# Making the rotary tables on GpSimd, and copying the first sequence's turned tokens on ScalarE, in a macaron block

## The chip, the cores and the metric

The kernel runs on one core of a Trainium2 chip. A core has five engines that run side by side, each through its own list of instructions in a fixed order: TensorE (PE: matrix products and transposes, with its weight loads shown apart as PEld), VectorE (DVE), ScalarE (ACT), GpSimd (POOL) and SyncE (SP), which here only issues DMAs. An engine waits for another by semaphores. Products land in PSUM, eight banks of 128 x 512 float32; everything else stands in SBUF, whose 128 partitions are the rows of every tile.

The metric is the device time of one execution in microseconds (us). Before the change it is 1862.89, the median of three runs (1862.62 to 1865.09).

## The reference

Eight sequences of 512 tokens with 128 channels pass through a macaron block: half an FFN block, an attention with latent keys, and the same FFN block by half again.

```python
x = x + 0.5 * ffn(layernorm(x))
x = x + latent_attention(layernorm(x))       # 16 heads of 8
x = x + 0.5 * ffn(layernorm(x))

def layer(x, ...):                           # ffn runs two of these
    h = shift_token(x)                       # second half of the channels from one token before
    q, k, v = split(h @ wqkv)                # 8 heads of 64
    q = l2norm(q) * qs;  k = l2norm(k) * ksc
    q, k = rotary_xpos(q, k)                 # q*cos*scale + rotate_half(q)*sin*scale; k by 1/scale
    x = x + local_attention(q, k, v) @ wo    # windows of 64, each sees itself and the one before
    h = layernorm(shift_token(x)) * lg + lb
    a, g = split(h @ w1 + b1)
    return x + (a * gelu(g)) @ w2 + b2
```

All of it is float32.

## The kernel before

The kernel has three parts: `ffn("f0")`, the first FFN half with two layers; `latent_attention()`; and `ffn("f1")`, the second FFN half. In an FFN half each of the 16 pairs of a layer `l` and a sequence `b` goes through `shift` (the tokens are normalized in layer 0, transposed, and copied with the channels' second half one token later), then for each of its four blocks `i` of 128 tokens through `begin`, `turn`, `scores`, `turn_probabilities`, `values` and `residual`, and at the end through `feed_forward`.

**Order by a planner.** Nothing of an FFN half is issued where it is written. Each piece of work is a step with a kind, an engine, a cost in microseconds, a rank, and what it reads, writes and holds. `Plan.run` (L159) then simulates the five engines: it looks at the 110 steps of the main row with the lowest ranks (and 40 of each side row), works out when each could start by the costs, takes the engine that can start first, and gives it, among its steps that can start by then, the one with the lowest rank. The order in which steps are picked is the order in each engine's list. The rank of a step is 100 times its place in the sequence of blocks (block `i` of the sequence numbered `s` has place 4s + i) plus an offset by kind from `PLACE` (L23). A step that needs a result of another engine starts 0.2 us later than it, with 0.1 more behind a PSUM access. The plan doesn't know the time of the first load, 5.4 us on the chip.

**The first steps.** The planner's steps that the prediction speaks of are these, with offset and planned cost:

- `ist`, `inr`, `inn`, `ina`: statistics on DVE (L488 to L490), an inverse root on ACT (L471, L472), a correction of it on POOL (L475 to L478) and the four normalizing products on DVE (L496), which write Y.
- `sh` (-500): four transposes of Y into one PSUM bank on PE (L508).
- `sd` (-790, DVE, 0.62): the bank's first 64 rows into the tile hT (L524). `sp`: a column of zeros on POOL. `sa` (-690, ACT, 0.5): the other 64 rows, one column later (L532).
- `qk0`, `qk1`, `v` (-320, -240, -19, PE): the projections of hT (L546), each into a bank of its own. There are four such banks.
- `sq0`, `sq1` (-480, -390, ACT): squares of a projection (L572), for the norm.
- `cs0`, `cs1` (-570, -360, DVE, 1.25): the two rotary products, with the cosine table (L556) and with halves exchanged by the sine table (L559). They read the bank and the table `("tab", l, s)`.
- `ad0`, `ad1` (-190, -430, POOL, 1.28): their sum (L580).
- `tb` (-450, DVE, 1.2): a rotary table. There are four, by layer `l` and by `t` for queries and keys; each multiplies the constant rotary factors, 128 x 256, by the heads' scale (L350), and the sine factors in two halves of 128 x 128 (L354). Their place is 2l, so the ranks are -450 for layer 0 and -250 for layer 1. All four read the tile `tables_u`, into which SP loads the scales and the rotary factors (L985, L990; 512 KB for the latter).
- `ld` at place 4 and `lw` (rank 100): once `tables_u` is free, its room, the only buffer of the ring `r_u`, takes seven small weights of the latent stage (L1027). Six products on PE (L1041) and their copies on DVE (L1047) make three matrices of them.

At the end of the first half, the first steps of the latent stage (`latent_begins`) are planned into the last sequences as a side row: memsets, projections, and DMAs that spread heads over partitions (`spread`, L1275). They borrow buffers of the FFN, among them the ring `ge` of the Gelu's results.

Of the kernel before, what the change touches and what calls it, by code (L numbers as in the profile page):

```python
# [188 lines left out]
def kernel(  # L189
# [21 lines left out]
    nc = tc.nc  # L211
# [35 lines left out]
    def load_tokens(b):  # L247
        nc.sync.dma_start(out=X[:, b], in_=x[b].rearrange("(n p) c -> p n c", p=P))
# [9 lines left out]
    def load_layer(l):  # L258

        yield lambda: nc.sync.dma_start(  # L260
            out=wo_sb[l], in_=wo[l].rearrange("(n p) c -> p n c", p=P)
        )
        yield lambda: nc.sync.dma_start(out=w1_sb[l], in_=w1[l])
        for c in range(NHC):
            yield lambda c=c: nc.sync.dma_start(
                out=w2_sb[l][: hsz[c], c], in_=w2[l, c * P : c * P + hsz[c], :]
            )
        yield lambda: nc.sync.dma_start(out=b2_sb[l], in_=b2[l].partition_broadcast(P))
# [54 lines left out]
    def mask_parts():  # L323

        for name, pattern, sign, op, fill in MASKS:
            yield lambda name=name: nc.gpsimd.memset(masks[name], 0.0)
            for g in range(4):
                rows = masks[name][quadrant(g)]
                yield lambda rows=rows, pattern=pattern, sign=sign, op=op, fill=fill: (
                    nc.gpsimd.affine_select(  # L330
                        out=rows, in_=rows, pattern=pattern, compare_op=op, fill=fill, base=0,
                        channel_multiplier=sign,
                    )
                )
        for k in range(2):
            yield lambda k=k: nc.gpsimd.memset(rows_sb[:, k], float(k))
# [10 lines left out]

    def rotary_table(l, s, rot_sb, scales):
        t, g = tabs[l], scales[:, s, l]
        nc.vector.tensor_mul(  # L350
            t[:, 2 * s], rot_sb[:, 2 * s], g.unsqueeze(1).to_broadcast([P, NB, DH])
        )
        for lo, fr in ((0, HD), (HD, 0)):
            nc.vector.tensor_mul(  # L354
                t[:, 2 * s + 1, :, lo : lo + HD],
                rot_sb[:, 2 * s + 1, :, lo : lo + HD],
                g[:, fr : fr + HD].unsqueeze(1).to_broadcast([P, NB, HD]),
            )
# [46 lines left out]
    def flat(t):  # L405
        return t.rearrange("p a b -> p (a b)") if len(t.shape) == 3 else t
# [5 lines left out]
    def ffn(tagname, last):  # L412
        plan = Plan(tc, nc)

        def step(kind, engine, cost, at, *args, **kw):
            return plan.step(kind, engine, cost, 100 * at + PLACE[kind], *args, **kw)

        PE, ACT, DVE, POOL, SP = range(5)
# [63 lines left out]
        def norm(k, w, src, dst, reads, writes, slots):  # L482

            st, mv, rs, ns, nt = (Slot(r) for r in (r_st, r_mv, r_rs, r_ns, r_nt))

            def stats():
                for i in range(NB):
                    nc.vector.bn_stats(st[:, i], src()[:, i])  # L488
                    nc.vector.bn_aggr(mv[:, i], st[:, i])
                nc.vector.tensor_scalar(rs.tile, mv[:, :, 1], LN_EPS, None, ALU.add)  # L490

            first, newton = root(rs, ns, nt)

            def apply():
                for i in range(NB):
                    nc.vector.tensor_scalar(  # L496
                        dst()[:, i], src()[:, i], mv[:, i, 0:1], ns[:, i : i + 1],
                        ALU.subtract, ALU.mult,
                    )

            step(w + "st", DVE, 1.6, k, stats, reads, [rs], [st, mv, rs] + slots)
            step(w + "nr", ACT, 0.45, k, first, [rs], [ns], [rs, ns])
            step(w + "nn", POOL, 0.9, k, newton, [rs, ns], [(ns, 1)], [rs, ns, nt])
            step(w + "na", DVE, 1.15, k, apply, [(ns, 1)] + reads, writes, [mv, ns] + slots)

        def transposes(src, dst):
            for i in range(NB):
                nc.tensor.transpose(dst[:, i * P : (i + 1) * P], src(i), ident)  # L508
# [3 lines left out]
        def shift(l, b, k):  # L512

            y = [("Y", b, i) for i in range(NB)]
            if l == 0:
                norm(k, "i", lambda: X[:, b], lambda: Y[:, b], [("X", b)], y, [])
            tp, hT = Slot(mm), Slot(r_hT)
            half = C // 2
            step(
                "sh", PE, 0.5, k, lambda: transposes(lambda i: Y[:, b, i], tp),  # L520
                y + ([("W", l)] if l else []), [tp], [tp], 0.1,
            )
            step(
                "sd", DVE, 0.62, k, lambda: nc.vector.tensor_copy(hT[:half, :], tp[:half, :]),  # L524
                [tp], [(hT, 0)], [tp, hT], 0.1,
            )
            step(
                "sp", POOL, 0.1, k, lambda: nc.gpsimd.memset(hT[half:, 0:1], 0.0),
                [], [(hT, 1)], [hT],
            )  # L530
            step(
                "sa", ACT, 0.5, k, lambda: nc.scalar.copy(hT[half:, 1:T], tp[half:, 0 : T - 1]),  # L532
                [tp], [(hT, 2)], [tp, hT], 0.1,
            )
            seqs[l, b] = hT, Slot(r_kT), Slot(r_V2), Slot(r_V)
# [429 lines left out]
        def load_step(k, what, writes=(), slots=(), after=3.0):  # L965
            step("ld", SP, 0.5, k, what, [], writes, slots, after)

        def first_loads():

            tables_u = Slot(r_u)  # L970
            size = 4 * NB * DH

            def rotary():
                return flat(tables_u.tile)[:, :size].rearrange(
                    "p (f n d) -> p f n d", f=4, n=NB
                )

            def scales():
                return flat(tables_u.tile)[:, size : size + 2 * L * DH].rearrange(
                    "p (s l d) -> p s l d", s=2, l=L  # L980
                )

            for t, scale in enumerate((q_scale, k_scale)):
                load_step(
                    0, lambda t=t, scale=scale: nc.sync.dma_start(  # L985
                        out=scales()[:, t].rearrange("p l d -> p (l d)"),
                        in_=scale.rearrange("l d -> (l d)").partition_broadcast(P),
                    ), [tables_u], [tables_u],
                )
            load_step(0, lambda: nc.sync.dma_start(out=rotary(), in_=rot), [tables_u], [tables_u])  # L990
            for l in range(L):
                for t in range(2):
                    step(
                        "tb", DVE, 1.2, 2 * l,
                        lambda l=l, t=t: rotary_table(l, t, rotary(), scales()),
                        [tables_u], [("tab", l, t)], [tables_u],
                    )
            load_step(0, lambda: nc.sync.dma_start(out=cols_sb, in_=cols), [("W", 0)])
            for what in load_layer(0):
                load_step(1, what, [("W", 0)])  # L1000
            for b in range(1, B):
                load_step(NB * b, lambda b=b: load_tokens(b), [("X", b)])
            load_step(
                NB * 3, lambda: nc.sync.dma_start(out=wqkv_sb[1], in_=wqkv[1]), [("W", 1)]
            )
            for what in load_layer(1):
                load_step(NB * 4, what, [("W", 1)])
            latent_weights()
            for what in mask_parts():
                step("lb", POOL, 0.65, 5, what, [], ["masks"])  # L1010
# [224 lines left out]
        if last:  # L1235
            plan.row = 0
            latent_ends()
            plan.row = 1
        else:
            first_loads()  # L1240
        for s, (l, b) in enumerate([(l, b) for l in range(L) for b in range(B)]):
            shift(l, b, NB * s)
            for i in range(NB):
                at = (l, b, i, NB * s + i)
                begin(*at)
                turn(*at)
                scores(*at)
                turn_probabilities(*at)
                values(*at)
                residual(*at)  # L1250
            feed_forward(l, b, NB * s)
# [418 lines left out]
```

## Time and profile before

| | |
|---|---|
| median of three runs | 1862.89 us |
| the profiled execution: time, span | 1861.75, 1860.0 us |
| busy share of the span: PE, PEld, DVE, ACT, POOL | 94%, 63%, 74%, 75%, 53% |
| mean granted PE clock | 0.982 |
| PE busy in the stretches 0 to 50, 50 to 100, 100 to 150, 150 to 200 us | 28.39, 45.11, 46.30, 48.40 us |
| chain that ended last, by engine | PE 59%, DVE 16%, ACT 13%, POOL 6%, issue 4% |
| L350 (table by cosine factors, DVE), 4 times | 0.41 us each, first 10.8, last 27.1 |
| L354 (half a table by sine factors, DVE), 8 times | 0.28 us each |
| L524 (first half of hT, DVE), 32 times | 0.68 us each |
| L532 (second half of hT, ACT), 32 times | 0.58 us each |
| end of the Gelu of the first, second, last sequence of the first half | 138.34, 182.46, 766.44 us |

The busy shares are means over parts with different limits; PE's share in particular counts matmuls that overlap, and a busy PE need not be at its peak. Times of the trace count from the span's start. The chain that ended last goes back from the last instruction, at each step to what released it; its shares say on which engine the time was spent that set the end.

### The profile page before, as it was taken

To read this page: it belongs to the slowest core of one execution; us is meant where nothing else is said; L and a number is where in the kernel's file an instruction comes from. 1 tells how busy PE (TensorE), PEld (TensorE's weight loads), DVE (VectorE), ACT (ScalarE), POOL (GpSimd) and SP (SyncE) were. 2 spreads that over 40 slices of the span, in tenths; PEclk is the share of its full clock that TensorE was granted. 3 is DMA by queue.
4 is the path that set the end of the run, shared out by engine and by line. 5 is a ranking of instruction groups with operands and counts; after the bars stand their busy time and mean duration, and the time that the engine had idled before them with its cause. 6 is when DMAs were issued, how large, how long until landed. Compare 5 with 4: busy or idle time off the path is not lost.

```text
span 1860.0 us, 50912 instructions
## 1 busy us (share of the span) xinstructions
PE 1742.7 (94%) x19860; PEld 1175.8 (63%) x19860; DVE 1367.5 (74%) x2886; ACT 1388.9 (75%) x3911; POOL 988.6 (53%) x1685
## 2 busy tenths in 40 slices
PE   5999999999999989899999998989999999999998
PEld 2556666666666656477777764656666666666666
DVE  7787877777777777567677647888877777777754
ACT  3878878888888877227677666878888888888875
POOL 5876766666666666100000016867666666666651
PEclk9999999999999999769999999999999999999999
DMA  3211111111111111100000000111111111111110
GB/s 107 51 33 30 30 24 24 24 26 25 24 24 24 26 24 24 29 6 23 16 17 15 15 3 19 27 24 29 26 24 24 26 28 24 30 31 35 29 33 24
DMA packets 51999, 50.03 MB, mean 27 GB/s; under 512 B 22790, under 2 KB 34736, under 8 KB 51760
## 3 DMA queue, kind: packets, MB, share of 16 engines
q1 hardware_dynamic: 51616, 46.00, 10.6%
q8 instruction: 158, 2.59, 0.6%
q10 hardware_dynamic: 144, 0.79, 0.1%
q14 instruction: 81, 0.66, 0.1%
HBM read 6.30 MB, written 2.10 MB: 5 GB/s over the span
## 4 chain that ended last, share of the span: by engine, by line
PE 59%; DVE 16%; ACT 13%; POOL 6%; issue 4%; DMA 1%; SPq 1%; ACTq 0%; DVEq 0%; POOLq 0%
PE mm_f L546 9%; PE mm_f L508 9%; PE mm_f L853 6%; ACT pr_f L696 5%; PE mm_f L895 4%; PE mm_f L762 4%; PE mm_f L786 4%; PE st L1401 4%; PE sc L1343 3%; PE lo L1418 3%; DVE c_f L556 3%; PE sc_f L679 3%; DVE s_f L559 3%; ACT sq_f L572 3%; PE mm_f L1343 2%
## 5 line engine op out<-in xcount | busy, mean ns | idle before, releaser
L696 ACT ACTIVATE pr_f<-sc_f,nm_f,q_f 128x128 f32<-128x128 f32 x1024 | 457.6, 474 | 5.4 <-DVE nm_f L689 3.9
L546 PE MATMUL mm_f<-wqkv,hT_f 128*128 128x512 f32 x768 | 391.7, 614 | 30.7 <-DVE s_f L559 14.0
L580 POOL TENSOR_TENSOR qk_f<-c_f,s_f 128x512 f32<-128x512 f32 x256 | 324.8, 1273 | 109.5 <-DVE s_f L559 99.3
L704 POOL TENSOR_TENSOR pr_f<-pr_f,rso_f 128x512 f32<-128x512 f32 x256 | 266.0, 1040 | 203.1 <-DVE rso_f L720 173.5
L556 DVE TENSOR_TENSOR c_f<-mm_f,tab 128x512 f32<-128x512 f32 x256 | 175.4, 685 | 82.8 <-ACT sq_f L572 36.7
L696 ACT ACTIVATION_READ_ACCUMULATOR pr_f<-sc_f,nm_f,q_f 128x1 f32 x1024 | 226.9, 222 | 0.0
L572 ACT ACTIVATE sq_f<-mm_f 128x512 f32<-128x512 f32 x256 | 153.4, 607 | 95.2 <-DVE s_f L559 58.4
L1412 ACT ACTIVATE pl<-st 128x512 f32<-128x512 f32 x280 | 156.2, 596 | 64.0 <-PE st L1401 55.0
L853 PE MATMUL mm_f<-fT_f,w 128*128 128x512 f32 (+1 forms) x384 | 191.9, 615 | 9.9 <-ACT ge_f L859 7.3
L508 PEld LDWEIGHTS mm_f<-ident,qk_f 128*128 128x128 f32 x1024 | 114.3, 141 | 126.1 <-POOL qk_f L616 51.9
L546 PEld LDWEIGHTS mm_f<-wqkv,hT_f 128*128 128x128 f32 x768 | 125.2, 193 | 101.0 <-issue 41.5
L508 PE MATMUL mm_f<-ident,qk_f 128*128 128x128 f32 x1024 | 159.8, 280 | 29.6 <-POOL qk_f L616 11.4
L688 DVE TENSOR_REDUCE nm_f<-sc_f 128x8 f32<-128x1024 f32 x128 | 155.2, 1213 | 43.4 <-PE sc_f L679 43.3
L762 PEld LDWEIGHTS mm_f<-pT_f,V_f 128*64 128x64 f32 (+1 forms) x4096 | 147.4, 136 | 60.4 <-issue 14.3
L762 PE MATMUL mm_f<-pT_f,V_f 128*64 128x64 f32 (+1 forms) x4096 | 179.8, 230 | 1.4 <-ACT kT_f L646 0.7
L559 DVE TENSOR_TENSOR s_f<-mm_f,tab 128x512 f32<-128x512 f32 x256 | 173.8, 679 | 0.0
L1433 POOL TENSOR_TENSOR X<-X,lon 128x128 f32<-128x128 f32 x27 | 12.0, 459 | 299.5 <-DVE lon L1427 299.3
L508 PE MATMUL mm_f<-ident,pr_f 128*128 128x128 f32 x1024 | 155.5, 279 | 13.3 <-ACT V_f L588 2.9
L508 PEld LDWEIGHTS mm_f<-ident,pr_f 128*128 128x128 f32 x1024 | 116.1, 141 | 78.8 <-POOL pr_f L704 33.5
L604 DVE TENSOR_REDUCE rn_f<-sq_f 128x16 f32<-128x1024 f32 x128 | 153.6, 1200 | 7.3 <-ACT sq_f L572 7.3
L786 PEld LDWEIGHTS mm_f<-wo,oT_f 128*128 128x128 f32 x1024 | 127.5, 191 | 39.2 <-issue 16.8
L786 PE MATMUL mm_f<-wo,oT_f 128*128 128x128 f32 x1024 | 140.5, 280 | 2.2 <-ACT oT_f L775 1.7
(168 smaller groups left out, 3855.0 us busy)
## 6 DMA issues: line engine op xcount, KB each, us to landing
V_f<-V_f SPq DMA_DIRECT2D x224, 128.0 KB
hs_f<-Y SPq DMA_DIRECT2D x32, 112.0 KB
X<-in_x_dram SPq DMA_DIRECT2D x8, 256.0 KB
out_dram<-hs_f SPq DMA_DIRECT2D x6, 256.0 KB
Y<-fl SPq DMA_DIRECT2D x32, 32.0 KB
kT_f<-fl SPq DMA_DIRECT2D x32, 32.0 KB
V_f<-fl SPq DMA_DIRECT2D x32, 32.0 KB
wqkv<-in_wqkv_dram ACTq DMA_DIRECT2D x1, 768.0 KB
```

Of the source, the lines that this page charges most:

```text
L508: nc.tensor.transpose(dst[:, i * P : (i + 1) * P], src(i), ident)
L546: nc.tensor.matmul(ps.tile, lhsT=hT[:, i * P : (i + 1) * P], rhs=wqkv_sb[l][:, at * INNER : (at + 1) * INNER], start=True, stop=True,)
L556: nc.vector.tensor_mul(c1.tile, psv, tabs[l][:, 2 * s, i].unsqueeze(1).to_broadcast([P, H, DH]))
L559: nc.vector.tensor_mul(s1.tile.rearrange("p h (t d) -> p h t d", t=2), psv.rearrange("p h (t d) -> p h t d", t=2)[:, :, ::-1], tabs[l][:, ...
L572: lambda s=s, ps=ps: nc.scalar.activation(sq[:, s], ps.tile, AF.Square),
L580: lambda s=s, c1=c1, s1=s1: nc.gpsimd.tensor_add(qk[:, s].rearrange("p (h d) -> p h d", d=DH), c1.tile, s1.tile),
L696: nc.scalar.activation(pr[:, h], sv[:, h % 2, h // 2], AF.Exp, bias=nm[:, h % 2, h // 2 : h // 2 + 1], scale=q8[:, h : h + 1], accum_out=s ...
L704: nc.gpsimd.tensor_mul(pr[:, heads], pr[:, heads], inv[:, heads].unsqueeze(2).to_broadcast([P, H // 2, P]),)
L762: nc.tensor.matmul(o[r * DH : (r + 1) * DH, u * P + w * WIN : u * P + (w + 1) * WIN], lhsT=(V2, V)[w][keys, i, h * DH : (h + 1) * DH], rhs ...
L786: nc.tensor.matmul(pw[:, :C], lhsT=oT[:, pr], rhs=wo_sb[l][:, pr], start=(pr == 0), stop=(pr == INNER // P - 1),)
L853: nc.tensor.matmul(ps[: hsz[c], :], lhsT=w1_sb[l][:, at + c * P : at + c * P + hsz[c]], rhs=fT.tile, start=True, stop=True,)
L1412: nc.scalar.activation(dst, bank, AF.Exp, scale=MSCALE)
```

## The change

The four tables are made on POOL with a planned cost of 1.3 and the place 4l, so the ranks are -450 for layer 0 and -50 for layer 1. In the first FFN half, layer 0, sequence 0, the step `sd` runs on ACT, with its planned cost of 0.62 unchanged. What is computed stays the same. Since the planner works from costs, engines and ranks, the whole order of the first FFN half is planned anew.

```diff
     def rotary_table(l, s, rot_sb, scales):
         t, g = tabs[l], scales[:, s, l]
-        nc.vector.tensor_mul(
+        nc.gpsimd.tensor_mul(
             t[:, 2 * s], rot_sb[:, 2 * s], g.unsqueeze(1).to_broadcast([P, NB, DH])
         )
         for lo, fr in ((0, HD), (HD, 0)):
-            nc.vector.tensor_mul(
+            nc.gpsimd.tensor_mul(
                 t[:, 2 * s + 1, :, lo : lo + HD],
...
             step(
-                "sd", DVE, 0.62, k, lambda: nc.vector.tensor_copy(hT[:half, :], tp[:half, :]),
+                "sd", DVE if last or l or b else ACT, 0.62, k,
+                lambda: (nc.vector.tensor_copy if last or l or b else nc.scalar.copy)(
+                    hT[:half, :], tp[:half, :]
+                ),
                 [tp], [(hT, 0)], [tp, hT], 0.1,
             )
...
                     step(
-                        "tb", DVE, 1.2, 2 * l,
-                        lambda l=l, t=t: rotary_table(l, t, rotary(), scales()),
+                        "tb", POOL, 1.3, 4 * l,
+                        lambda l=l, t=t: rotary_table(
+                            l, t, rotary(), scales()
+                        ),
                         [tables_u], [("tab", l, t)], [tables_u],
                     )
```

## The prediction

> **What bounds the kernel now.** I read three views in this order: the page's 40 slices, the busy time in stretches, and the timeline of the first 60 us with the chain of waits beside it. The slices tell where the change acts and what limits that place:
>
> ```profile
> PE   5999999999999989899999998989999999999998
> DVE  7787877777777777567677647888877777777754
> POOL 5876766666666666100000016867666666666651
> PEclk9999999999999999769999999999999999999999
> ```
>
> From the second slice on TensorE (PE) is full; only the first slice (46.5 us) has it at 5 tenths. In stretches of 50 us it is busy 28.39 us in the first, 45.11 in the second, 46.30 in the third and about 48 from the fourth on. So the two FFN halves run at PE's pace, and the time before that is a filling stretch in which PE waits for others. A microsecond won there, where all later work starts from, comes out at the end if the rest keeps its order. The timeline shows who is late in the filling stretch:
>
> ```profile
> 9.54 0.20 POOL L478 TENSOR_TENSOR ns_f<-ns_f,nt_f 128x4 f32<-128x4 f32 x1
> 9.78 1.11 DVE L496 TENSOR_SCALAR Y<-X,mv_f,ns_f 128x128 f32<-128x128 f32 x4 [1.70 <-POOL ns_f L478]
> 11.46 0.58 ACT L532 COPY hT_f<-mm_f 64x511 f32<-64x511 f32 x1 [2.91 <-PE mm_f L508]
> 12.07 0.68 DVE L524 COPY hT_f<-mm_f 64x512 f32<-64x512 f32 x1 [0.44 <-ACT hT_f L532]
> 16.94 1.27 POOL L580 TENSOR_TENSOR qk_f<-c_f,s_f 128x512 f32<-128x512 f32 x1 [7.20 <-DVE s_f L559]
> 18.31 0.69 DVE L556 TENSOR_TENSOR c_f<-mm_f,tab 128x512 f32<-128x512 f32 x1 [1.45 <-ACT sq_f L572]
> 27.15 0.41 DVE L350 TENSOR_TENSOR tab<-u_f 128x256 f32<-128x256 f32 x1
> 27.48 0.48 DVE L354 TENSOR_TENSOR tab<-u_f 128x128 f32<-128x128 f32 x2
> 27.89 0.68 DVE L524 COPY hT_f<-mm_f 64x512 f32<-64x512 f32 x1
> 28.61 0.29 PEld L546 LDWEIGHTS mm_f<-wqkv,hT_f 128*128 128x128 f32 x1 [0.83 <-DVE hT_f L524]
> ```
>
> Each line is start, length, engine, line, operation, and in brackets the idle time before it with what ended it. The reader is to see four things. GpSimd (POOL) is idle for 7.20 us just when the tables are made. The first sequence's two copies into hT run one after the other although they are on two engines. VectorE (DVE) idles 1.45 us before its second pair of rotary products, and then has no gap until 29.46. And the fourth table stands in that full stretch, ahead of the second sequence's copy, for which PE waits 0.83 us.
>
> **The change, part by part.**
>
> *The first sequence's copy.* Before, hT is whole at 12.07 + 0.68 = 12.75. After, ScalarE (ACT) does both: the first 11.46 to 12.04, the second right behind; two such ACT instructions in a row took 1.09 (L572 x2), so the second adds 0.51 and ends at 12.55. Gain 0.20; least 0, if PE, whose idle time before 12.86 is put down to issue, waits for something else.
>
> *The tables on POOL.* 4 x (one 128x256 and two 128x128) leave DVE. No table product on POOL is in the trace. POOL's broadcast product of 128x512 takes 1.04 (L616), a 128x4 one 0.20: 0.84 for 508 columns, hence 0.62 for 256 and 0.41 for 128, or 1.44 a table and 5.8 for four. By the dearer row, the 1.27 sum (L580), it is 0.73 + 2 x 0.46 = 1.65, 6.6 for four. Both fit into the 7.20 idle before 16.94, so POOL's cost is 0 there; without the cover the first sums would come later by what sticks out. Queued behind the tables on POOL are these sums, on which the first query transposes wait.
>
> *Contention at the start.* The tables now follow POOL's 9.54 instruction at once, beside DVE's four normalizing products (9.78). The second sequence shows what such company costs: there the four took 2.32 (23.71) instead of 1.11, one of them 1.30 instead of 0.34, while POOL's two sums ran at their usual 1.27. Here POOL's pieces are shorter: the four DVE products wait for some 0.62 + 0.41 + 0.41 at most one by one, less the overlap. I take 0.62 + 0.41 = 1.03 plus 0.03 of hand-over, a loss of 1.06 against 1.21 measured there; 0, if the table's 512 KB land only after 10.9, and 2.1 if all four wait.
>
> [...]
>
> *DVE's order.* The list order is planned from costs and ranks. Without tables on DVE its first rotary product (rank -570) is planned at 8.5 (its matmul ends at 8.2 in the plan, and signals take 0.3) instead of 9.4, when the third table was done. At its end the planner then finds the key product of block 0 ready (-360) and block 1's (-470) not yet. Before, block 1's came second and had to wait for the third square: 18.31. Block 0's key product needs the second square, at 16.65 + 0.60 = 17.25, so starts about 17.28. Gain 1.03, least 0.
>
> *The fourth table at 27.15.* It takes 27.89 - 27.15 = 0.74 in DVE's full stretch and on PE's path (0.83 wait). Gain 0.74, least 0.
>
> *What the tables release.* The tables' source tile is also the room of seven small latent weights. Their DMAs are issued from 27.99, when the fourth table ends; after, from about 16 to 17.5. The SP queue has nothing else due between, so these seven are moved past nothing but their own wait. Their six products on PE and six copies on DVE now stand at 41 to 47:
>
> ```profile
> 44.07 1.07 PE L1041 MATMUL mm_f<-u_f 64*64 64x128 f32 x6
> 46.21 0.48 PE L1041 MATMUL mm_f<-u_f 64*128 64x128 f32 x2 [1.08 <-DVE u_f L1047]
> 46.63 2.91 PE L546 MATMUL mm_f<-wqkv,hT_f 128*128 128x512 f32 x4
> ```
>
> From 44.07 to 46.63 PE has nothing but these products and the wait for their copy. Earlier, at 20 to 32, PE has idle times of 3.10, 0.68, 0.46 and 0.77 that could take them. Gain 2.56 if they go there; a loss of up to 1.0 (0.32 + 0.18 + 0.48, what they cost in the chain now) if they stand in the way there. I take the gain, since the row shows an empty PE and the loads come 11 us sooner.
>
> *The clock.* The granted clock is 0.50 from about 47.5 to 50.9, and those four matmuls take 2.91; four at the 0.43 spacing of 17 to 18.3 take 1.72. Closing the gap before them may spare 1.2; opening another may cost as much. A gap of 2.10 at 38.29 did not lower the clock, so I take half the gain, 0.60.
>
> **The sum:** -0.20 + 1.06 - 1.03 - 0.74 - 2.56 - 0.60 = -4.07. The profiled execution took 1861.75 (span 1860.0 and 1.75 around it), which gives 1857.7. It lies 1.14 under the median of the runs, so against the median: **1858.8**. With every term at its better end the sum is -0.2 - 1.0 - 0.7 - 2.6 - 1.2 = -5.7; with only the contention, +1.1: 1857.2 to 1864.0 for this case.
>
> That the rest keeps its order I read from the trace itself. The exponential table is reloaded after each sequence's Gelu. From the first to the thirteenth of these the first half takes 672.03 - 138.34 = 533.69, the second, with quite another beginning, 1770.78 - 1236.79 = 533.99. Different heads fall into the same rhythm.
>
> **Rivals.**
>
> *A: the latent products only move (no more than 0.9 won).* For it: DVE is busy 2.00 of 2.00 us at 22 to 24 and at 26 to 28, where their copies would now fall. Against it: they need 0.2 to 0.3 each. Without the last two terms the sum is -0.91: 1862.0.
>
> *B: slower, at the hand-over to the latent stage.* The plan's times shift, and at 745 to 770, where the last sequences mix with the latent stage's spreading DMAs, the order can fall otherwise. The price is on record there:
>
> ```profile
> 761.24 1.28 ACT L859 ACT_TABLE_LOAD   x1 [5.50 <-DMA kT_f<-ge_f]
> ```
>
> A Gelu waits 5.50 for a buffer that a DMA still reads. One more such wait with the gain of A: 1862.9 - 0.9 + 5.5 = 1867.5. It decides from an added wait of 4.6. For it: the clock is at 0.50 from 782 to 822, so a later start there is not made up. Against it: the equal rhythm above.
>
> *C: slower at the head.* All four normalizing products wait (2.1), POOL's tables stick out by 1.0 over the first sum, PE's longer gap costs another spell of half clock (1.2, the price above), and nothing but the copy's 0.2 is won: +4.1, 1867.0. It decides if PE's first projection starts later than 14 and the first sum later than 18. For it: a gap of 3.10 before 23.94 is followed by a clock of 0.50 from 24 to 30. Against it: before the first projections the clock is 1.00 throughout.
>
> *D: faster twice.* The hand-over loses its 5.50 wait as well: 1858.8 - 5.5 = 1853.3. For it and against it: as in B, with the sign turned.
>
> *E: the change does not do what it says:* the tables are planned on POOL so late that the rotary products wait. Ranks -450 and -50 and a free POOL speak against it; I give it nothing of its own.
>
> **How the numbers follow.** 0.2% of 1862.9 is 3.7 us, about what a measurement of this kernel can tell from no change; the bounds are 1859.2 and 1866.6. Forecast 0.42, of which 0.30 ends below 1859.2 and 0.12 inside. A 0.17, inside. B 0.25, of which 0.24 above and 0.01 inside. C 0.08, of which 0.06 above and 0.02 inside. D 0.08, below. Faster 0.38, same 0.32, slower 0.30. The range reaches to B and some way to D: 1854.5 to 1869.0; the forecast's own is 1857.2 to 1864.0.
>
> **What would show it.** Right: L350 and L354 on POOL between 9.8 and 17; two ACT copies into hT ending by 13.6; DVE's normalizing products longer than 1.11; the third rotary pair before the second sequence's statistics; the latent weights' DMAs at 16 to 18 and L1041 before 40; the first Gelu reload some 4 us before 138.34; 533 to 534 us from there to the thirteenth. Wrong: a first reload at or after 138.34, another rhythm, or a gain at the first reload that is gone when the latent stage begins; then the plan's order, and not these costs, made the time.

## The result, and the profile after

| | before | after |
|---|---|---|
| median | 1862.89 us (1860.34 to 1865.36, 19 executions) | 1866.46 us (1862.00 to 1869.06, 19 executions) |
| ratio, 95% interval | | 1.0018, 1.0011 to 1.0025 |
| profiled execution: time, span | 1861.75, 1860.0 us | 1865.15, 1863.4 us |
| mean granted PE clock | 0.982 | 0.980 |
| end of the first Gelu | 138.34 us | 140.61 us |
| first to thirteenth Gelu | 533.69 us | 534.58 us |

The change cost 3.4 us (1.0011 to 1.0025 of 1862.89 is 2.0 to 4.7 us) where 4.07 were to be won. It was measured twice more, in e5 and e17 below: 1.0013 (1.0003 to 1.0023) and 0.9998 (0.9985 to 1.0010). The three together, weighted by their intervals, give 1.0013, which is 2.4 us. The first and the third differ by more than their intervals allow (1.0011 to 1.0025 beside 0.9985 to 1.0010), so the doubt is nearer 2 us than 1 either way.

The slices of the page after, the same four rows as were shown of before (busy tenths in 40 slices of 46.6 us, and the granted clock):

```profile
PE   5899999999999999899999998999999999999998
DVE  6777877777778777667767646888877777777754
POOL 6876766666666666100000015867666666666651
PEclk8999999999999999869999999999999999999999
```

DVE has lost a tenth in the first slice and POOL won one, as the change says. But the second slice of PE is down to 8 tenths, and the clock of the first slice too. The timeline after, with the lines that answer to those of before:

```profile
9.87 1.68 DVE L496 TENSOR_SCALAR Y<-X,mv_f,ns_f 128x128 f32<-128x128 f32 x4 [1.70 <-POOL ns_f L478]
10.22 0.82 POOL L350 TENSOR_TENSOR tab<-u_f 128x256 f32<-128x256 f32 x1 [0.40 <-DMA u_f<-in_rot_dram]
12.11 0.58 ACT L525 COPY hT_f<-mm_f 64x512 f32<-64x512 f32 x1 [3.48 <-PE mm_f L508]
12.71 0.58 ACT L535 COPY hT_f<-mm_f 64x511 f32<-64x511 f32 x1
15.53 0.87 POOL L354 TENSOR_TENSOR tab<-u_f 128x128 f32<-128x128 f32 x2
16.93 2.22 ACT L575 ACTIVATE sq_f<-mm_f 128x512 f32<-128x512 f32 x4 [3.65 <-DVE s_f L562]
18.12 0.69 DVE L559 TENSOR_TENSOR c_f<-mm_f,tab 128x512 f32<-128x512 f32 x1 [1.29 <-ACT sq_f L575]
27.09 1.11 PE L508 MATMUL mm_f<-ident,Y 128*128 128x128 f32 x4 [1.16 <-DVE s_f L562]
28.85 0.68 DVE L525 COPY hT_f<-mm_f 64x512 f32<-64x512 f32 x1 [0.62 <-ACT hT_f L535]
```

The tables are on POOL and end at 15.53 + 0.87 = 16.40, before the first sum needs it (16.91). The normalizing products took 1.68 beside them instead of 1.11. The second rotary pair starts at 18.12, hardly earlier than the 18.31 of before, because the four squares now wait for DVE's first pair (3.65 us, ended by its s_f, in the row of 16.93), which reads the bank of the first square and was picked ahead of it. The second sequence's transposes wait 1.16 for a bank, so its copy lands at 28.85 instead of 27.89 although no table stands ahead of it any more.

Next the same stretches of both kernels: start:end, length, then busy time and instructions of PE, PEld, DVE, ACT and POOL, the granted clock, the DMA share and GB/s. First before, then after:

```profile
24.00:28.00 4.00, 2.86 (x9) 1.84 (x10) 4.00 (x10) 1.16 (x2) 2.13 (x3) 0.50 0.00 0
28.00:32.00 4.00, 3.23 (x8) 1.04 (x6) 3.10 (x6) 0.58 (x1) 1.09 (x1) 0.69 0.17 43
32.00:38.00 6.00, 3.51 (x13) 1.48 (x10) 5.76 (x15) 4.07 (x12) 4.01 (x10) 1.00 0.27 62
```

```profile
24.00:28.00 4.00, 2.85 (x6) 1.07 (x6) 4.00 (x8) 0.00 (x0) 2.13 (x3) 0.50 0.18 74
28.00:32.00 4.00, 2.28 (x3) 0.50 (x2) 3.34 (x6) 0.88 (x2) 1.57 (x2) 0.50 0.00 0
32.00:38.00 6.00, 5.57 (x14) 3.00 (x14) 4.63 (x15) 4.06 (x13) 2.52 (x9) 0.60 0.20 46
```

Both kernels fall to half clock at 23 to 24 us. Before comes back at 30.48; after stays down to 36.82. In steps of 3.41 us from the fall, PE is busy for 2.20 and 3.20 us in before, and for 2.09, 1.52, 2.64 and 3.41 us in after: in both, full clock came back behind the first step that was filled to over nine tenths (3.20 and 3.41).

Last, score groups, each opened by four mask products, with other PE work between them, before and then after. The first line of each fence is the third group, the last one the seventh:

```profile
51.96 0.41 PE L669 MATMUL sc_f<-band,ident 64*64 64x512 bf16 x4
...
55.92 2.18 PE L762 MATMUL mm_f<-pT_f,V_f 64*64 64x64 f32 x32
...
61.47 0.41 PE L669 MATMUL sc_f<-band,ident 64*64 64x512 bf16 x4
...
65.64 0.66 PE L508 MATMUL mm_f<-ident,Y 128*128 128x128 f32 x4
66.23 0.41 PE L669 MATMUL sc_f<-band,ident 64*64 64x512 bf16 x4
...
83.71 0.41 PE L669 MATMUL sc_f<-band,ident 64*64 64x512 bf16 x4
```

```profile
52.05 0.41 PE L672 MATMUL sc_f<-band,ident 64*64 64x512 bf16 x4 [1.59 <-ACT pr_f L699]
...
58.78 0.41 PE L672 MATMUL sc_f<-band,ident 64*64 64x512 bf16 x4 [1.10 <-ACT pr_f L699]
...
59.90 2.12 PE L765 MATMUL mm_f<-pT_f,V_f 64*64 64x64 f32 x32
...
65.17 0.41 PE L672 MATMUL sc_f<-band,ident 64*64 64x512 bf16 x4
...
68.20 0.98 PE L508 MATMUL mm_f<-ident,Y 128*128 128x128 f32 x4
...
86.07 0.41 PE L672 MATMUL sc_f<-band,ident 64*64 64x512 bf16 x4
```

The groups may be compared only where PE has the same work behind it. At the fourth group the changed kernel is 2.69 us ahead (61.47 - 58.78), but that is no gain: there it has yet to do 32 value products (59.90), 8 residual products and 8 transposes that before has done. At the third group the counts are equal, but for four transposes that have changed places with four others, and the two kernels are level (51.96, 52.05). At the seventh the counts are equal to the last product, and after is 2.36 behind (83.71, 86.07). In between the order differs: before turned the third sequence (the transposes of Y) ahead of its fifth group, after turns it behind. The lists of the two programs differ only in their beginning: those of PE in the first 371 of 15779 instructions, which end just behind the seventh group, those of DVE in the first 156 of 2891. From there they are the same.

### The profile page after: what moved, and what is told of

The parts are those of the page before. It is cut to its first block, busy times and chain, and to the rows that moved or that the text cites. A ratio compares the mean times of both kernels' runs of the same rounds, so it can differ in the third digit from the quotient of the medians.

```text
span 1863.4 us, 50919 instructions
## 1 busy us (share of the span) xinstructions
PE 1745.3 (94%) x19860; PEld 1176.8 (63%) x19860; DVE 1367.1 (73%) x2873; ACT 1389.0 (75%) x3912; POOL 994.4 (53%) x1697
## 4 chain that ended last, share of the span: by engine, by line
PE 56%; DVE 18%; ACT 14%; POOL 6%; issue 4%; DMA 1%; SPq 1%; ACTq 0%; DVEq 0%; POOLq 0%
PE mm_f L549 9%; PE mm_f L508 8%; PE mm_f L856 6%; ACT pr_f L699 6%; PE mm_f L898 4%; PE mm_f L765 4%; PE st L1406 4%; PE sc L1348 4%; PE mm_f L789 3%; PE lo L1423 3%; DVE c_f L559 3%; DVE s_f L562 3%; PE sc_f L682 3%; ACT sq_f L575 3%; DVE nm_f L691 2%
```

## The experiments

**One part at a time.** e1 has the tables on POOL and the copy on DVE; e2 the copy on ACT and the tables on DVE. e3 and e4 part the plan from the work: e3 runs the tables on POOL in the order planned for before, e4 runs them on DVE in the order planned for after.

```diff
 # e3, against before; the step "tb" stays DVE, 1.2
-        nc.vector.tensor_mul(
+        nc.gpsimd.tensor_mul(
             t[:, 2 * s], rot_sb[:, 2 * s], g.unsqueeze(1).to_broadcast([P, NB, DH])
         )
...
 # e4, against after; the step "tb" stays POOL, 1.3
-        nc.gpsimd.tensor_mul(
+        nc.vector.tensor_mul(
             t[:, 2 * s], rot_sb[:, 2 * s], g.unsqueeze(1).to_broadcast([P, NB, DH])
         )
...
```

> The tables are made on GpSimd as in the change; the first sequence's copy stays on VectorE. TensorE's list is the one of the changed kernel, instruction for instruction. Theory order (the time is lost because the planner lays out the first 60 us anew): 2 to 4 us slower than before, first Gelu reload at 140 to 141 as after (140.61). Theory engine (the time is lost because GpSimd's tables hold up VectorE's normalizing products at 10 us): also slower, by 0.5 to 2.3. Theory copy (ScalarE's two copies in a row are what costs): as before, reload near 138.3.

> The first sequence's two copies are on ScalarE; the tables stay on VectorE. TensorE's list is again that of the changed kernel, instruction for instruction. Theory order: 2 to 4 us slower than before, reload at 140 to 141, though GpSimd makes no table. Theory engine: as before within 0.5, reload at 138.0 to 138.6.

> The planner is told what it was told before (VectorE, 1.2), so every list but for the table instructions is that of before; the table instructions themselves are put on GpSimd. Theory order: no slower than before; the wait at 10 us (about 0.6) and the 0.74 won at 27 us roughly cancel, reload at 137.5 to 138.8. Theory engine: 0.5 to 2.3 slower, reload at 139 to 141.

> The planner is told what the change tells it, so TensorE's, ScalarE's and SyncE's lists are those of the changed kernel, but the table instructions are put on VectorE, at the place where they are planned. Theory order: 2 to 4 us slower than before, as after, reload at 140 to 141.5. Theory engine: as before within 0.5, reload near 138.3.

| | ratio to before, 95% interval | first Gelu ends | half clock between 18 and 142 us |
|---|---|---|---|
| e1 | 1.0005, 0.9994 to 1.0017 | 140.06 | 17.1 us |
| e2 | 1.0001, 0.9990 to 1.0012 | 140.41 | 13.7 |
| e3 | 0.9998, 0.9987 to 1.0008 | 139.33 | 20.5 |
| e4 | 1.0000, 0.9990 to 1.0010 | 140.34 | 17.1 |

(before has 13.7 us of half clock there, after 17.1.) e1 and e2 both give TensorE's new list exactly, so either part alone turns the order over, and the Gelu comes 1.7 to 2.1 us later than in before whether the tables are on POOL or not. In e3 it comes 0.99 later, in the range that was written for theory engine: the fourth table at 25.54 holds up the second sequence's normalizing products (2.90 instead of 2.32), and there are two half-clock spells more than in before. None of the medians is told from before, where theory order had 2 to 4 us for e1, e2 and e4; so a loss of 2 us at the first Gelu is not a sure loss at the end.

**The clock kept up by spare matmuls.** In all seven profiles of a kernel with one or both parts of the change and no fill (after, e1 to e5, e17), half clock runs from 23 to 25 us up to 36 to 39, for 13.65 us; in before and its repeat e6 it lasts 6.8. e3 is among the seven, so the new order is not the only way to the longer stretch. e7 and e8 give PE bf16 products of 128 x 512 into an unused bank after some of its first steps, 25 of them in before and 22 in after, where it would wait. They compute nothing that is used.

```diff
+        FILL = {7: 10, 8: 2, 9: 1, 11: 3, 12: 2, 16: 7}      # e7; e8: {7: 6, 8: 2, 9: 4, 10: 5, 11: 3, 12: 2}
...
+            for _ in range(FILL[n]):
+                nc.tensor.matmul(
+                    spare[0][:, 0].rearrange("p (u w) -> p u w", w=P), lhsT=ident16,
+                    rhs=bands[1].unsqueeze(1).to_broadcast([P, 4, P]),
...
```

> The changed kernel once more, beside before and the next kernels on one chip. Theory order plus contention: first Gelu reload at 139.8 to 140.8 (1.7 for the order, up to 0.6 more if the rotary factors land before VectorE's normalizing products); the time 1.5 to 4 us over before. If the 3.6 us of the first comparison are mostly scatter: less than 1.5 over before.

> The kernel of before, profiled once more, to see how far a profile's own stages scatter. If the first stage is fixed by the lists: first Gelu reload at 138.3 within 0.4. If the spells of half clock fall by chance: their sum over the execution differs from 68 us by several times 3.4, and the span goes with it at about 0.3 us per us.

> Before, with 25 matmuls of 128x512 bf16 into a bank that nothing else uses yet, put into TensorE's idle times of the first 40 us, to keep its clock up; the lists are otherwise those of before. Theory clock (what the lists cost in the head is the spell of half clock that their gaps bring): no spell at 23 to 38, first Gelu reload 1 to 3 us sooner, 135.3 to 137.3. Theory gaps (the waits themselves cost, whatever the clock): reload within 0.5 of 138.3, or later by what the added matmuls take.

> The changed kernel with 22 such matmuls in its idle times of the first 34 us; its lists are otherwise its own. Theory clock: no spell at 23 to 38, reload at the same time as that of before filled, within 0.7. Theory gaps: it stays 1.5 to 2.3 later than that of before filled.

e5: 1.0013 (1.0003 to 1.0023), first Gelu at 139.65. e6: span 1861.4, first Gelu at 136.85. e7: 0.9991 (0.9982 to 0.9999), 136.42, and no half clock between 18 and 60. e8: 1.0003 (0.9994 to 1.0012), 138.24, with one spell of 3.4 us at 38 and one at 89. The fill helps both kernels, but the new order still ended its first Gelu 1.82 us behind the old. By what was written for it, that spoke against the clock as the whole cause, and I looked for the rest in the order.

One profile is a poor measure of the first Gelu, though: e6 is before again and ends it 1.49 sooner than before did, against a forecast of 0.4 either way. What holds is the time from the third score group to the end of the first Gelu in the profiles that have no half clock in between:

| order | from the third score group to the end of the first Gelu |
|---|---|
| of before | e6 85.42, e15 85.50, e18 85.68 us |
| of after | e2 87.32, e9 87.33, e5 87.35, e16 87.42, e17 87.43 us |

(e9 and e15 to e18 follow below.) So at full clock the new order costs 1.6 to 2.0 us up to there, whichever engine makes the tables (in e2 it is DVE) and with the fill or without it. About half of that is lost by the seventh group (32.2 to 32.4 us from the third, against 33.2), the other half behind it.

**Repairing the order.** e9 lets the first square be picked ahead of the first rotary pair; e10 makes six projections of the first sequence wait for the second sequence's transposes, to give those their bank; e12 makes the fourth sequence's statistics wait for the third sequence's normalizing products, as before had it; e14 brings that one item the other way round into before. All four have a fill: that of e7 in e14, that of e8 in e9 and e12, one of 24 products in e10.

```diff
 # e9
-                    f"sq{s}", ACT, 0.5, k,
+                    f"sq{s}", ACT, 0.5, k - (1 if not last and l == b == i == s == 0 else 0),
 # e10
+                for at in [(0, 0, 3, 0), (0, 0, 3, 1)] + [(0, 0, i, 2) for i in range(NB)]:
+                    early[at].needs.append(turned)
 # e12
+                    norms[3][0].needs.append(norms[2][1])
 # e14
+                    norms[2][1].needs.append(norms[3][0])
```

> The changed kernel with the matmuls in its idle times, and with the first square put into the program ahead of the first rotary pair, so that the pair waits for the square and not the square for the pair; every engine's list is that of after filled. Theory squares (the new order costs because ScalarE's four squares now stand behind VectorE's first pair): squares from 15, second rotary pair at 17.3 to 17.5 instead of 18.1, first Gelu reload 0.5 to 1.5 sooner than the 138.24 of after filled. Theory bank (it costs because the second sequence's transposes come behind one more projection and wait for a bank): reload within 0.4 of 138.24.

> The changed kernel with the matmuls in its idle times, and with the fourth block's projections and the value projections of the first sequence planned behind the second sequence's transposes, as they stood before; the order after it is planned anew. Theory bank: the transposes at 25 to 26, the second sequence's copy done before 28.5, reload 1 to 2 sooner than 138.24. Theory squares: transposes still after 26.5, reload within 0.5 of 138.24.

> The changed kernel with the fill of e8, and one condition more for the planner: the fourth sequence's statistics wait until the third sequence's normalizing products are placed on VectorE, which is how they stood before the change (there 64.17 and 69.94 us; in the changed kernel 65.30 and 67.59). Theory order (some 1.4 us of the loss lie in the new order, where the third sequence starts late): the third sequence's transposes at about 65.1 instead of 66.6 us of e8, the first Gelu reload at 136.2 to 137.2 instead of 138.24 with as many half-clock spells, and the median 1 to 2 us under that of e13. Theory clock (the order costs nothing; only the number of 3.4-us half-clock spells, which differs from execution to execution, makes the difference): the transposes move and the reload, set right by 0.75 us for each spell, stays where e8 had it, the median within 1 us of e13.

> e8 again, beside e12 and e15 on one chip. Theory order: ratio to e15 1.0005 to 1.0012, reload 1 to 2 us behind e15's with as many spells. Theory clock: ratio to e15 within 0.0005 of 1; where the reload is later, the profile shows one or two spells more between 18 and 142 us.

> The kernel before with the fill of e7, and the third sequence's normalizing products placed behind the fourth sequence's statistics, as in the changed kernel. Theory order: 1 to 2 us over e15, third transposes at 66.3 or later instead of 64.78. Theory clock: the median of e15 within 1 us.

> e7 again. Both theories: 0.9985 to 0.9998 of the kernel before. With e13 it gives the new order's cost where the clock of the first 40 us is kept up in both: theory order 1 to 2 us, theory clock under 1 us.

e9 did at the place what was foretold: the second rotary pair came at 17.20, which is the 17.28 of the prediction, and the second sequence's transposes at 26.18. Yet the first Gelu ended at 138.73, 0.49 later than in e8. e10 brought the transposes to 25.00, and the Gelu came at 142.31. So mending the lateness between 17 and 29 us, plain as it is in the timeline, brought no earlier Gelu in either. Each of the two ran once: 1864.72 and 1863.91 us, beside a median of 1863.62 for before on that chip.

e12 was to win 1 to 2 us and lost: 1.0007 (0.9998 to 1.0016) where e13, the same without its edit, has 0.9986 (0.9975 to 0.9997). DVE and then POOL in e12, from the timeline, and last DVE in e13:

```profile
63.95 2.77 DVE L517 TENSOR_SCALAR Y<-X,mv_f,ns_f 128x128 f32<-128x128 f32 x4
```

```profile
63.85 1.27 POOL L608 TENSOR_TENSOR qk_f<-c_f,s_f 128x512 f32<-128x512 f32 x1 [0.19 <-DVE rso_f L748]
65.08 1.04 POOL L732 TENSOR_TENSOR pr_f<-pr_f,rso_f 128x512 f32<-128x512 f32 x1
```

```profile
66.27 1.16 DVE L517 TENSOR_SCALAR Y<-X,mv_f,ns_f 128x128 f32<-128x128 f32 x4
```

Its mean granted clock, 0.9829, is that of e13 (0.9827), so the loss is not the clock's. Moved ahead, the products ran beside POOL's sum and quotient and took 2.77 us instead of 1.16. The transposes of Y stayed where PE's list has them (66.67, in e13 66.88), and the maxima behind the moved statistics started a microsecond late (68.55 after 67.55). e14 came out at 0.9999 (0.9990 to 1.0007) beside e15's 0.9990 (0.9980 to 1.0000), with a median 1.98 us higher, as theory order had it (1 to 2); but its third transposes fell to 70.89, further than in any kernel of the new order. That the third sequence starts late in the new order is so in every run. Whether the normalizing products make it late is open: e14 speaks for it, e12 against it, and neither brought the third transposes to where the other order has them.

e13 and e15 were to answer the larger question, whether the new order is slower at the end where both have the fill: 0.9986 and 0.9990 say no. But e8 and e7, the same two kernels on another chip, gave 1.0003 and 0.9991. The pairs do not agree, and in the second the intervals barely meet (0.9994 to 1.0012, 0.9982 to 0.9999), so these four leave the question open.

**More fill.** e16 adds eight spare matmuls at 34 to 38 us, after which e8 and e13 had their one early spell. e17 and e18 are after and e7 again, on the same chip.

```diff
-        FILL = {7: 6, 8: 2, 9: 4, 10: 5, 11: 3, 12: 2}
+        FILL = {7: 6, 8: 2, 9: 4, 10: 5, 11: 3, 12: 2, 16: 5, 17: 3}
```

> The changed kernel with the fill of e8 and eight spare matmuls more in TensorE's idle times between 34 and 38 us, after which e8 and e13 had their one half-clock spell in the first 60 us (38 to 42). Theory clock: no half clock between 18 and 60 us, the mean granted clock of its runs at 0.983, as in e15; ratio to the kernel before 0.9982 to 0.9994, the median 2.5 to 4 us under e17 and within 1 us of e18. Theory order: the clock comes up likewise, and the median still lies 1 to 2 us over e18.

> The changed kernel a third time, beside the two filled ones. Both theories: ratio 1.0008 to 1.0022, mean granted clock 0.980, and in the profile half clock from 23 to 25 us on to 36 or 38 us, where the kernel before is back at full clock at 31.

> The kernel before with the fill of e7, a third time. Both theories: ratio 0.9983 to 0.9998 and mean granted clock 0.983; it is what e16 is measured against.

| | median | ratio to before, 95% interval | mean granted clock of its executions |
|---|---|---|---|
| before on that chip | 1865.51 us | | 0.9810 |
| e17, after | 1865.51 | 0.9998, 0.9985 to 1.0010 | 0.9818 |
| e18, before with fill | 1863.75 | 0.9985, 0.9973 to 0.9997 | 0.9828 |
| e16, after with more fill | 1861.33 | 0.9979, 0.9966 to 0.9993 | 0.9845 |

The stretches of e16 that answer to the two tables above:

```profile
24.00:28.00 4.00, 2.73 (x14) 1.17 (x12) 3.83 (x8) 0.58 (x1) 1.78 (x2) 1.00 0.31 129
28.00:32.00 4.00, 3.57 (x14) 1.59 (x14) 3.96 (x6) 1.89 (x4) 1.27 (x1) 1.00 0.15 35
32.00:38.00 6.00, 5.84 (x27) 2.77 (x26) 5.31 (x18) 3.73 (x14) 3.99 (x12) 1.00 0.29 67
```

There is no half clock in e16 between 18 and 760 us, and it is the fastest kernel of the study: 4.18 us under e17 (theory clock: 2.5 to 4) and 2.42 under e18 (theory clock: within 1; theory order: 1 to 2 over). That is the clock, which is the highest of all (0.9845), and not the order: from the third group to the Gelu e16 needs 87.42 us like the other kernels of the new order. In its profile the last Gelu of the first half ends 3.4 us behind that of e15 (765.46, 762.04), and neither has half clock between 16 and 759 us; its span is 0.4 us shorter all the same (1858.8, 1859.2), with three half-clock spells less from 759 on. That e17 is level with before on this chip was foretold by neither theory.

**Time against clock, over all executions.** Each timed execution comes with its mean granted clock. Of before 135 have it; by clock, without nine at the ends:

| mean granted clock | 0.978 | 0.979 | 0.980 | 0.981 | 0.982 | 0.983 |
|---|---|---|---|---|---|---|
| executions of before | 6 | 9 | 20 | 30 | 28 | 33 |
| mean time, us | 1869.28 | 1867.69 | 1865.66 | 1864.92 | 1864.24 | 1862.49 |

The scatter of one and the same kernel goes with the clock (correlation -0.85). A straight line through 298 executions of before and of ten other kernels, with a level for each chip and each kernel (e1, e2 and e4 share one), falls by 1.12 us (give or take 0.10) for each 0.001 of clock. One spell of 3.4 us at half clock takes 1.7 us of full clock away, 0.0009 of the mean, and so costs about 1.0 us. At equal clock that fit leaves these distances from before:

| kernel | us over before at equal clock, 95% interval |
|---|---|
| after (e5, e17) | 0.80, 0.19 to 1.41 |
| new order otherwise (e1, e2, e4 together) | 0.53, -0.08 to 1.13 |
| after with fill (e8, e13) | 0.65, 0.02 to 1.27 |
| after with more fill (e16) | 0.23, -0.67 to 1.13 |
| before with fill (e7, e15, e18) | 0.21, -0.33 to 0.75 |
| tables on POOL in the old order (e3) | -0.62, -1.50 to 0.26 |
| the item of order moved (e12; e14) | 3.48, 2.61 to 4.36; 1.13, 0.25 to 2.01 |

So at equal clock the change costs 0.2 to 1.4 us. POOL's work in the old order costs nothing that can be seen, which leaves the new order; its other rows are of the same size, though two of them reach zero. The 0.80 is less than the 1.6 to 2.0 us at the first Gelu; where the rest is made up was not looked for.

**The hand-over to the latent stage.** Every kernel but e11 spends 41 or 44 us at half clock from about 780 on. e11 puts two spare bf16 products behind each step of the maxima there, in before with fill.

```diff
+            times = 2 if kind == "lm" else FILL.get(n, 0)
```

> Before filled, and at the hand-over to the latent stage two matmuls of 128x512 bf16 more behind each of the 24 groups of maxima products, where the clock is at half for some 40 us while TensorE is never idle. If full-width matmuls bring the clock back up there: clock 1.0 for most of 785 to 822, the next stage 4 to 10 us sooner, 1853 to 1858. If the clock stays down: 24 x 2 x 0.43 = 20 us at most longer, 1870 to 1883.

1.0157 (1.0143 to 1.0171), 1893.27 us: 29.65 over before on that chip, and 10 above the worse of the two ranges. By the profile PE was busy without a gap, and the clock did not come:

```profile
785.00:821.00 36.00, 36.00 (x187) 17.18 (x188) 13.33 (x21) 0.00 (x0) 0.00 (x0) 0.50 0.00 1
```

Half clock lasted 75 us there, to 851.5. So the spare work is paid in full and more, and buys nothing; what holds the clock down there is not idle time that the profile shows, and stays open.

## Why the prediction was wrong

It forecast 1858.8 us and a gain. The measured 1866.46 lies inside its range (1854.5 to 1869.0) and within its 0.2%, on the other side of no change. By its steps:

- **The first sequence's copy**, -0.20. On ACT the two copies end at 12.71 + 0.58 = 13.29, with the pair at 1.18 and not 1.09. What it won can't be read alone, since the contention delays the start: the first projection came at 13.38 instead of 12.86, +0.52, where this term and that of the contention together said +0.86.
- **The tables on POOL**, 0. Right: 1.50 to 1.62 us a table (1.44 to 1.65 forecast), 6.18 for four, and no first sum waited.
- **Contention at the start**, +1.06. Right in kind, half in size: 1.68 - 1.11 = 0.57; 1.88 - 1.11 = 0.77 in e5, where the tables began at 10.15, and none in e1 and e17, where they began at 10.94 and 10.98, behind the products. In these four it went by when the 512 KB had landed. In after the third and fourth of the products took 0.75 and 0.49 instead of 0.34, and ended 0.08 and 0.09 behind the table products of 0.82 and 0.45 that POOL had begun ahead of them; in e12 the first two took 1.25 and 1.08 beside POOL's 1.27 and 1.04, and the other two 0.34 each.
- **DVE's order**, -1.03. Wrong: 0.19 (18.31 to 18.12). The key product did come second, but the planner also picked the first rotary pair ahead of the first square of the same bank, which I had not followed, and the squares moved from 14.94 to 16.93. e9 puts this right and has the pair at 17.20; from the third group to the Gelu it needs the same 87.33, so the term was wrong twice, for the place and for its worth.
- **The fourth table**, -0.74. It is gone from 27.15, and the copy behind it came 0.96 later all the same, since the transposes now wait for a bank.
- **What the tables release**, -2.56. This is the step that failed. The loads did come sooner (16.42 to 20.4), but the products did not go into PE's idle times at 20 to 32: they stand at 38.16 to 45.4, where they were at 41.22 to 46.7. At the third score group, with them done in both kernels, the changed one is level with before (52.05, 51.96); the 2.56 are not there. Then the replanned order itself costs time. The third sequence is turned behind the fifth group and no longer before it, and from the third group to the seventh after needs 34.02 us instead of 31.75, to the end of the Gelu 88.56 instead of 86.38, with one half-clock spell in each; without one it is 1.6 to 2.0 us (the table of e2 to e18). I had taken a gap at one place for a gain at the end, on the condition in the text, "if the rest keeps its order", and I tested that only from the first Gelu on, where it holds (534.58 beside 533.69), and not between 50 and 80 us. The prediction had named the sign of this: a first reload at or after 138.34, by which the plan's order and not these costs made the time. The text also had nothing else due on the SP queue; the fourth load of tokens and the second of wqkv now stand behind the seven loads (20.41 and 20.88, before 11.38 and 12.29). No wait for them shows in the trace up to 140 us.
- **The clock**, -0.60. Wrong in sign: 13.7 us of half clock in the first 60 us instead of 10.2. The spell at 47.5 that the term was about is gone, as forecast, though the repeat e6 of before hasn't it either. But I did not watch the stretch from 23 to 37, where the new order fills no step of 3.41 us before 33.4 (2.64 us at most) and stays two spells longer at half clock; e16, with spare work there, has none. Against rival C the text also set a clock of 1.00 ahead of the first projections. The view says so, but the record of the clock begins at 16.83, and the projections stand 0.85 us apart up to there and 0.43 after it, so up to there it was half.

The sum of it: of the 2.4 us that the three measurements give, about 0.8 stays at equal clock and goes to the order. The rest, about 1.6, is the clock's by estimate only, and the clock differed from chip to chip: 0.9801, 0.9802 and 0.9818 in the three. That the measured time lies inside the range is luck, since the range was drawn for other causes: it reaches up there for rival B's wait.

Of the rivals, C came nearest: slower at the head, with contention and another spell of half clock; it asked for a first projection after 14 and a first sum after 18, and neither happened (13.38, 16.91). A was right that the latent products only move. B and D did not happen: the Gelu's wait at the hand-over is 5.21 instead of 5.50.

```profile
764.11 1.28 ACT L862 ACT_TABLE_LOAD   x1 [5.21 <-DMA kT_f<-ge_f]
```

What stays open: which of the steps between 50 and 80 us puts the third sequence behind in the new order, where the 1.6 to 2.0 us of the first Gelu shrink to the 0.8 at equal clock, and why e16 had fewer half-clock spells than e18 after 800 us too, where their lists are the same.

## What to carry to other kernels

Where a planner or scheduler makes the order, two small edits give a new order, and a price taken from one gap holds only up to the next place where the order differs. Compare the two orders at places where the same work lies behind both: a lead at one instruction can be work that was put off. Where TensorE's clock falls and rises, read the granted clock of each short stretch beside its busy time, for a spell of 3.4 us at half clock cost about 1.0 us here, by the line above; and set the time of repeats against their mean clock before putting a 0.1% down to an edit. Spare matmuls in idle times of the filling stretch were worth more here than the edits: 1.0003, 0.9986 and, with eight more, 0.9979 for the change with them, 0.9991, 0.9990 and 0.9985 for the kernel before with them.

## What the runs showed of the hardware

Half clock came in spells of 3.4 us and its whole multiples: 3.4, 6.8, 10.2, 13.65, 41.0, 44.4 and, in e11, 75.1 us in 20 profiles, but for the last one of each, which the end of the execution cuts off. At 30.48 in before and 36.82 in after, full clock came back behind a step in which PE was busy for 3.20 and 3.41 of 3.41 us. At the hand-over in e11 it did not: there PE was 100% busy for 36 us at 0.50. By how much of the step is filled the cases do not part: 91% in e6 (28.59 to 32.00) had full clock behind it, and 93% in e9 (37.04 to 40.45) had not.

In the 3.4 us ahead of the fall at 23 us PE was busy for 0.60 us in before and 1.51 in after, so the clock fell there without a wholly idle step. Its longest gap between 13 and 24 us was 3.10 in before and 1.91 in after (ahead of the transposes at 22.56).

The record of the clock begins at 15.6 to 18.9 us in the 20 profiles (at 16.83 in before, 16.34 in after). Up to there the first projections stand 0.85 us apart, from there 0.43, in before as in after. So full clock first came 3.1 us apart in two executions of one kernel (15.84 in e15, 18.91 in e18). In e18 the fourth square started 1.50 us later than in e15 (19.59, 18.09), and the first of the probabilities still 1.20 later (42.37, 41.17), with no half clock in between in either: a profile's time at the first Gelu carries such differences with it.
